# Cross attention on one core: output rows in other tiles, batch 0's sums in another order, and Wv loaded by halves of its columns

## The chip, the cores and the metric

The kernel runs on one core of a Trainium2 chip. The metric is the device time of one execution in microseconds (us). "Before" is the median of three runs, 992.72 us (991.76 to 993.55).

A core has five engines with queues of their own, each working in its queue's order: TensorE (PE in the profile; its weight loads are PEld), VectorE (DVE), ScalarE (ACT), GpSimd (POOL) and SyncE (SP), which here only issues DMAs. ACT and POOL issue some DMAs too. TensorE writes its results into PSUM banks, from which VectorE or ScalarE must copy them before the bank is used again.

## What is computed

There are 16 batches of 100 query rows of 640 columns (x) and 722 context rows of 384 columns. The last 4 context rows are the "ca" tokens; the other 718 are "enc". There are 8 heads of 80 columns. Cut to what matters:

```python
query = hidden_states @ Wq                  # 100 x 640
keyt, valt = enc @ Wk, enc @ Wv             # 718 x 640
hs = _mha(query, keyt, valt)
ca_q1 = jnp.einsum('btc,th->bch', ca, Wq_ca)[:, indices, :]
ca_hs1 = _mha(ca_q1, residual, residual)    # 100 queries on the batch's own x
ca_q2 = ca_hs1 @ Wq
ca_hs2 = _mha(ca_q2, ca @ Wk_ca, ca @ Wv_ca)
out = (hs + ca_hs2) @ Wout + b_out + residual
```

## The kernel before

Everything is float32. A loop of 16 steps handles one batch each, as a pipeline: in step b the scores, softmax and weighted values of batch b are computed, the keys of batch b + 1 are prepared, and the output rows that batch b - 1 has completed are projected with Wout. From the loop on, the order on TensorE, VectorE and GpSimd is the order in which the lines stand in the program; ACT's instructions are placed by the tile framework, with some tied behind a named instruction (`tc.issue_after`).

**Start.** Before the loop SP loads enc of batch 0, the small weights, Wq transposed, x, Wk transposed (into `kT`, L210) and Wq (into `wq_in`, L215), in that order. ACT issues Wv's four DMAs (L195): the first 128 rows in two halves of 320 columns, the other two blocks of 128 rows whole.[...] TensorE first computes the values of batch 0 (`first_values`, L277), then a fold of Wq with the token keys (L841, L864), transposes Wk (L886) and computes batch 0's keys (`first_keys`, L446). VectorE rearranges Wq into `wq_sb` (L897 to L904), and copies half of the transposed Wk into `wk_sb` (L889).

**Values and keys by blocks.** From batch 1 on a value or key product is made by the class `Blocks` with eleven block products instead of twelve, on sums and differences of the operands. It has two halves: `first_half` issues four products into four PSUM banks; the first bank is copied by ACT (L317), the others are added to that copy by VectorE (L319, L321, L323). `second_half` adds seven products into the same banks, with one ACT copy (L333) and three VectorE sums (L335, L337, L339). Key blocks `ka` and `kb` write `kT`; `last_keys` (L446) makes the fifth chunk, in two banks that `ka` has used.

**Scores and softmax.** `scores` (L505) makes the scores of 718 keys x 800 columns (8 heads x 100 queries) in three groups of PSUM banks; ACT copies them into `st` (L515). The greatest score of a column over all keys is found by VectorE (`larger`, then class `Maximum`): a transpose (L548), three reductions (L550, L553, L560), a spreading copy (L571 on ACT in two pieces, or L576 on VectorE) and a transpose back (L579). `subtract` (L976) takes it off the three pieces of `st`; `exponential` (L986) follows on ACT. The same class serves the first attention of the tokens (`softmax1`, on `e1`, with L663 and the exponential L667).

**Weighted values and the end of a step.** For each half g of the heads TensorE multiplies `st` with the values (L1117), 48 products into one bank `a_ps`, in two column tiles (64 and 36 queries). VectorE divides by the sums (L1125, L1127), which frees the bank, and adds the tokens' part `hs2` (L1133). `hs2` is made by GpSimd in `values2` (L736, L743), which is made to wait for the last subtraction of the step. Batch 1's second group of scores reuses the two `a_ps` banks of batch 0.

**Batch 0's step** (L996 to L1049) has an order of its own, because no batch stands before it: `Maximum` up to its third stage, `ka.first_half`, the rest of `Maximum`, the first subtraction, `kb.first_half`, two more subtractions, the second halves, `last_keys`, `values2`, and then the whole of `second.softmax1` and its exponential, all ahead of the division of batch 0's own result.

**Output rows.** `OC` (L32) cuts the 1600 output rows into tiles: eleven of 128 rows, one of 92 (rows 1408 to 1499) and one of 100 (the last batch). A tile is projected in the step after the one that completes it. `Last.transpose` transposes a batch's 100 rows (L780) and ACT copies them into the tile's `hsT` (L789); two `hsT` buffers exist. `Last.load` loads x's rows into `xn` and GpSimd adds the bias (L771). `Last.project` (L804) has ten products of 320 columns for a tile, VectorE adds `xn` (L816) and SP stores (L822; for the last tile each half by itself, L820). Step 15 projects two tiles of batch 14; after it the last batch's tile is projected with five chunks of 128 columns, of which the first two are transposed before the last head's products (L1114).

Of the kernel before, what the change touches and what calls it, by code (L numbers as in the profile page):

```python
# [8 lines left out]
F32 = mybir.dt.float32  # L9
AF = mybir.ActivationFunctionType  # L10
ALU = mybir.AluOpType
# [3 lines left out]
B, S, H = 16, 100, 640  # L15
# [3 lines left out]
P = 128  # L19
HC = H // P  # L20
CC = CAD // P
# [7 lines left out]
ROWS = NH * S  # L29
NB = ROWS // 32  # L30

OC = [(r, min(P, (B - 1) * S - r)) for r in range(0, (B - 1) * S, P)] + [((B - 1) * S, S)]  # L32
HT = NH * T

QC = [(0, 64), (64, S)]
# [10 lines left out]
for h in range(NH):  # L46
    lo = h * D
    while lo < (h + 1) * D:
        c = lo // P
        hi = min((h + 1) * D, (c + 1) * P)  # L50
        PIECES.append((h, c, lo - h * D, lo - c * P, hi - lo))
        lo = hi
# [39 lines left out]
def kernel(  # L92
# [18 lines left out]
    nc = tc.nc  # L111
# [4 lines left out]
    main = ctx.enter_context(tc.tile_pool(name="main", bufs=1))  # L116
# [7 lines left out]
    def psum4(name, n=4):  # L124
        return [
            ps4.tile([P, 512], F32, tag="ps4", name=f"{name}_{j}") for j in range(n)
        ]
# [15 lines left out]
        return main.tile([P, H], F32, tag="hs", name=name)  # L143

    def hsT_tile(name):
        return main.tile([P, HC, P], F32, tag="hsT", name=name, bufs=2)

    def xn_tile(name):
        return main.tile([P, H], F32, tag="xn", name=name, bufs=3)
# [41 lines left out]
    enc = enc_tile("enc_0")  # L191
    for c in range(CC):
        in_order(nc.sync.dma_start(out=enc[0][:, c, :P], in_=enct[0][:, c, :P]))
        for cols in [slice(0, H // 2), slice(H // 2, H)] if c == 0 else [slice(0, H)]:
            nc.scalar.dma_start(  # L195
                out=wv_sb[:, c, cols], in_=wv[c * P : (c + 1) * P, cols]
            )
# [553 lines left out]
    hsTs = {}  # L751

    class Last:
# [7 lines left out]
        def load(self):  # L761

            self.xn = {}
            for r, (lo, n) in enumerate(OC):
                if not self.b * S < lo + n <= (self.b + 1) * S:
                    continue
                xn = self.xn[r] = xn_tile(f"xn_{r}")
                nc.sync.dma_start(
                    out=xn[:n], in_=x.rearrange("b s n -> (b s) n")[lo : lo + n]
                )  # L770
                nc.gpsimd.tensor_tensor(xn[:n], xn[:n], bias[:n], ALU.add)  # L771

        def transpose(self, chunks=[(0, HC)]):
            b, hs = self.b, self.hs
# [19 lines left out]
        def project(self, chunks=range(HC)):  # L794
            for r, xn in self.xn.items():
                lo, n = OC[r]
                if chunks[0] == 0:
                    if self.split:
                        self.o_ps = [psum1(f"o_ps_{r}_{k}") for k in range(2)]
                    else:  # L800
                        self.o_ps = psum4(f"o_ps_{r}", 2)
                o_ps = self.o_ps
                for c, k in [(c, k) for k in range(2) for c in chunks]:
                    nc.tensor.matmul(  # L804
                        o_ps[k][:n, : H // 2],
                        hsTs[r][:, c, :n],
                        wout_sb[:, c, k * (H // 2) : (k + 1) * (H // 2)],
                        start=(c == 0),
                        stop=(c == HC - 1),
                    )  # L810
                if chunks[-1] < HC - 1:
                    continue
                o_v = out.rearrange("b s n -> (b s) n")[lo : lo + n]
                for k in range(2):
                    cols = slice(k * (H // 2), (k + 1) * (H // 2))
                    nc.vector.tensor_tensor(  # L816
                        xn[:n, cols], o_ps[k][:n, : H // 2], xn[:n, cols], ALU.add
                    )
                    if self.split:
                        nc.sync.dma_start(out=o_v[:, cols], in_=xn[:n, cols])  # L820
                if not self.split:
                    nc.sync.dma_start(out=o_v, in_=xn[:n])  # L822

    act, dve = nc.scalar.copy, nc.vector.tensor_copy

# [125 lines left out]
    for b in range(B):  # L951
# [32 lines left out]
        def exponential(i, behind):  # L984
            with tc.issue_after(behind.ins):
                return nc.scalar.activation(st[i], st[i], AF.Exp, scale=SCALE)  # L986
# [36 lines left out]
        if b == 0:  # L1023
            now.scores2()
            now.softmax3()
            for i, halves in ((3, (0, 1)), (5, (0,)), (5, (1,))):
                first_values(i, e_in, (act, act), halves)
            second.scores1()
            weight_sums([wv2[:, j] for j in range(3)], wv_raw, [3])
            second_next, enc_next = loads()  # L1030
            ka, kb = (key_blocks(b + 1, i, enc) for i in range(2))
            top = Maximum(most, f"{b}", lambda: copied)
            top.go(3)
            ka.first_half(psum4(f"room1_{b}"))
            top.go()
            subtract(0)
            exponential(0, top.spreading)
            kb.first_half()
            subtract(1)
            exponential(1, kb.copies[0])  # L1040
            less = subtract(2)
            ka.second_half()
            exponential(2, ka.copies[1])
            kb.second_half()
            final = last_keys(b + 1, enc)
            now.values2(less)
            second.load()
            second.softmax1()
            second.exponentials1(final[-1])  # L1049
        else:  # L1050
            last.transpose()
            va, vb, vc = (values(b, i, e_in) for i in range(NP))
            top = Maximum(most, f"{b}", lambda: va.copies[1])
            if b + 1 < B:
                second.scores1(seen)
                last.load()
                ka, kb = (key_blocks(b + 1, i, enc) for i in range(2))
            else:
                last.load()
                mine.load()  # L1060
            va.first_half()
            top.go(2)
            vb.first_half(psum4(f"room_{b}"))
            top.go(1)
            va.second_half()
            now.scores2()
            vb.second_half(lambda: top.spreading, top.go)
            subtract(0)
            vc.first_half()
            exponential(0, vc.copies[0])  # L1070
            now.softmax3()
            if b == B - 1:
                now.values2()
            subtract(1)
            if b + 1 < B:
                ka.first_half(psum4(f"room1_{b}"))
                less = subtract(2)
                vc.second_half()
                second_next, enc_next = loads()
                exponential(1, vc.copies[1])  # L1080
                ka.second_half()
                exponential(2, ka.copies[1])
                now.values2(less)
                second.load()
                last.project()
                kb.first_half()
                second.softmax1(3)
                final = last_keys(b + 1, enc)
                kb.second_half()
                second.softmax1()  # L1090
                second.exponentials1(kb.copies[1])
            else:
                exponential(1, vc.copies[0])
                subtract(2)
                last.project()
                vc.second_half()
                exponential(2, vc.copies[1])
# [10 lines left out]
        for g in range(2):  # L1108
            a_ps = psum1(f"a_ps_{b}_{g}")
            a_v = a_ps[:S, : 4 * (D + 1)].rearrange("p (h e) -> p h e", e=D + 1)  # L1110
            for h in range(4 * g, 4 * g + 4):
                if b == B - 1 and h == NH - 1:

                    mine.transpose([(0, 2)])  # L1114
                for i in range(len(KC)):
                    for lo, hi in QC:
                        nc.tensor.matmul(  # L1117
                            a_v[lo:hi, h % 4],
                            st[i // 2][:, i % 2, h * S + lo : h * S + hi],
                            block(i, h // 4)[:, h % 4],  # L1120
                            start=(i == 0),
                            stop=(i == len(KC) - 1),
                        )
            rs = small.tile([S, 4], F32, tag="rs", name=f"rs_{b}_{g}")
            nc.vector.reciprocal(rs.unsqueeze(2), a_v[:, :, D : D + 1])  # L1125
            cols = slice(4 * g * D, 4 * (g + 1) * D)
            nc.vector.tensor_tensor(  # L1127
                hs[:S, cols].rearrange("p (h d) -> p h d", h=4),
                a_v[:, :, :D],
                rs.unsqueeze(2).to_broadcast([S, 4, D]),  # L1130
                ALU.mult,
            )
            added = nc.vector.tensor_tensor(  # L1133
                hs[:S, cols], hs[:S, cols], hs2[:, cols], ALU.add
            )
        last = mine

    last.project(range(2))
    last.transpose([(2, HC)])
    last.project(range(2, HC))  # L1140


# [48 lines left out]
```

## Time and profile before

| what | us |
|---|---|
| median of three runs | 992.72 |
| the profiled execution | 992.88 |
| its span | 991.2 |
| VectorE busy, TensorE granted clock over the span | 666.9, 1.00 |
| start of batch 0's weighted values (a_ps) and of batch 1's scores | 97.38, 104.27 |
| weighted values of batch 15: start | 973.56 |
| end of the last TensorE instruction | 987.48 |

Times in the profile are counted from the span's start. A line of the timeline gives start, duration, engine, line of the program, operation, output and inputs, sizes and count; in brackets stands how long the engine was idle before it and what released it. A float32 product appears as two matmul records and two weight loads. The chain of waits is followed back from the last instruction: at each step to what released it. A list of waits gives the waiting instruction, what it waited for, the total, the number of times and the longest.

### The profile page before, as it was taken

Reading aid. Unit: us, or ns where it says so; the run is one execution under the profiler, and the core shown is the slowest. Engines: PE = TensorE matmul, PEld = TensorE weight load, DVE = VectorE, ACT = ScalarE, POOL = GpSimd, SP = SyncE. Lnnn points to the kernel's source line nnn. Section 1 sums busy time; section 2 is a strip of 40 time slices with the busy share of each in tenths; the row PEclk is TensorE's granted clock in tenths of the full one; section 3 lists DMA queues with packets and bytes.
Section 4 is the critical chain, followed back from the end, with each engine's and each line's share of the span. In section 5 each row is a group of like instructions: output and inputs, shape, how many; then the busy total and the mean of one; then the engine's idle time right before and its main releaser. Section 6 shows DMA issues by size and latency. Waiting matters only on the chain.

```text
span 991.2 us, 25050 instructions
## 1 busy us (share of the span) xinstructions
PE 980.1 (99%) x10945; PEld 747.5 (75%) x10945; DVE 666.9 (67%) x1229; ACT 312.9 (32%) x599; POOL 489.4 (49%) x439
## 2 busy tenths in 40 slices
PE   8999999999999999999999999999999999999998
PEld 6785869677696777868678686886869778696775
DVE  1358893967739587576946768468683876739782
ACT  1243342414334143333313233132332424324241
POOL 4467762565606546272653717446471564704513
PEclk9999999999999999999999999999999999999999
DMA  8651111120302202011120211102021030200101
GB/s 270 205 155 58 44 51 44 40 101 9 112 3 73 70 8 87 24 65 58 52 68 24 80 42 52 68 23 84 12 77 43 8 110 2 84 29 1 44 2 34
DMA packets 18015, 59.93 MB, mean 60 GB/s; under 512 B 2126, under 2 KB 8278, under 8 KB 14386
## 3 DMA queue, kind: packets, MB, share of 16 engines
q1 hardware_dynamic: 14658, 40.46, 12.6%
q0 software_dynamic: 2512, 16.72, 5.4%
q8 instruction: 86, 1.41, 0.6%
q10 hardware_dynamic: 736, 1.15, 0.4%
q14 instruction: 23, 0.19, 0.1%
HBM read 54.07 MB, written 4.26 MB: 59 GB/s over the span
## 4 chain that ended last, share of the span: by engine, by line
PE 93%; DMA 2%; SPq 1%; DVE 1%; POOL 1%; issue 1%; ACT 0%; ACTq 0%; DVEq 0%; POOLq 0%
PE room L302 19%; PE v_ps L302 18%; PE s_ps L505 12%; PE a_ps L1117 10%; PE k_ps L302 10%; PE o_ps L804 7%; PE kT_ps L446 7%; PE q_ps L420 7%; PE y_ps L611 2%; SPq L210 1%; DMA wq<-in_wq 1%; PE z_ps L674 1%; PE hst_ps L780 1%; PE v_ps L277 1%; DMA wv_sb<-in_wv 1%
## 5 line engine op out<-in xcount | busy, mean ns | idle before, releaser
L646 POOL TENSOR_TENSOR e<-ca,g 100x800 f32<-100x800 f32 x64 | 97.8, 1538 | 317.1 <-PE v_ps L302 299.3
L736 POOL TENSOR_TENSOR hs<-vb,p 100x640 f32<-100x640 f32 x64 | 83.8, 1320 | 132.9 <-DVE st L976 100.9
L302 PE MATMUL v_ps<-wv_sb,enc 128*128 128x320 f32 (+1 forms) x480 | 149.1, 433 | 0.0
L515 ACT COPY st<-s_ps 128x400 f32<-128x400 f32 (+1 forms) x192 | 80.5, 505 | 120.8 <-PE s_ps L505 120.8
L302 PEld LDWEIGHTS v_ps<-wv_sb,enc 128*128 128x128 f32 (+1 forms) x480 | 84.9, 179 | 41.1
L1117 PEld LDWEIGHTS a_ps<-v,st 128*64 128x64 f32 (+3 forms) x3072 | 109.0, 125 | 7.1 <-issue 6.5
L1117 PE MATMUL a_ps<-v,st 128*64 128x81 f32 (+3 forms) x3072 | 112.0, 233 | 0.7 <-issue 0.7
L986 ACT ACTIVATE st<-st 128x1600 f32<-128x1600 f32 (+1 forms) x48 | 73.8, 1538 | 103.2 <-DVE st L976 103.2
L976 DVE TENSOR_TENSOR st<-st,over 128x1600 f32<-128x1600 f32 (+1 forms) x48 | 105.3, 2197 | 0.0
L505 PE MATMUL s_ps<-qp,kT 32*128 32x100 f32 (+1 forms) x3072 | 98.5, 263 | 1.7 <-DVE hs L1127 1.1
L505 PEld LDWEIGHTS s_ps<-qp,kT 32*128 32x128 f32 (+1 forms) x3072 | 95.4, 179 | 3.7 <-issue 2.3
L653 POOL TENSOR_TENSOR e<-e,e 100x800 f32<-100x800 f32 x48 | 90.3, 1881 | 3.8
L302 PE MATMUL k_ps<-enc,wk_sb 128*128 128x359 f32 x240 | 82.6, 465 | 1.3 <-ACT v L284 1.0
L302 PE MATMUL room<-enc,wk_sb 128*128 128x359 f32 x240 | 82.2, 464 | 0.0
L991 DVE TENSOR_TENSOR most<-most,st 128x800 f32<-128x800 f32 (+1 forms) x64 | 64.4, 1007 | 25.6 <-ACT st L515 24.5
L743 POOL TENSOR_TENSOR hs<-hs,hs 100x640 f32<-100x640 f32 x48 | 73.9, 1540 | 3.8
L302 PE MATMUL room<-wv_sb,enc 128*128 128x320 f32 x240 | 74.4, 432 | 0.0
L804 PE MATMUL o_ps<-wout_sb,hsT 128*128 128x320 f32 (+2 forms) x260 | 72.2, 433 | 0.5 <-ACT hsT L789 0.5
L420 PEld LDWEIGHTS q_ps<-xT,wq_sb 128*128 128x128 f32 x400 | 67.9, 190 | 2.1 <-issue 0.5
L420 PE MATMUL q_ps<-xT,wq_sb 128*128 128x200 f32 x400 | 69.1, 333 | 0.0
L446 PE MATMUL kT_ps<-enc,wk_sb 128*128 128x359 f32 x210 | 68.8, 465 | 0.1
L1125 DVE RECIPROCAL rs<-a_ps 100x4 f32<-100x4 f32 x32 | 5.8, 181 | 92.1 <-PE a_ps L1117 91.9
(134 smaller groups left out, 1537.0 us busy)
## 6 DMA issues: line engine op xcount, KB each, us to landing
enc<-in_enct SPq DMA_DIRECT2D x15, 1077.0 KB
vb<-va_d POOLq DMA_DIRECT2D x16, 1000.0 KB, 6.7
xT<-in_xt SPq DMA_DIRECT2D x8, 500.0 KB
xn<-in_x SPq DMA_DIRECT2D x11, 320.0 KB
out<-xn SPq DMA_DIRECT2D x11, 320.0 KB
ca<-in_cas SPq DMA_DIRECT2D x16, 156.2 KB
wout_sb<-in_wqt SPq DMA_DIRECT2D x1, 1600.0 KB
wq<-in_wq SPq DMA_DIRECT2D x5, 320.0 KB
```

The source lines that it names most:

```text
L302: nc.tensor.matmul(bank[: left.shape[1], : right.shape[1]], left, right, start=(first and i == 0), stop=(last and i == len(products) - 1), ...
L420: nc.tensor.matmul(q_ps[:, : 2 * S].rearrange("p (j s) -> p j s", j=2), wq_sb[:, c, n * P : (n + 1) * P], xT[:, :, c, :], start=(c == 0), ...
L446: nc.tensor.matmul(k_ps[:, :KH], w, a, start=(c == 0), stop=(c == CC - 1))
L505: nc.tensor.matmul(s_ps[r][:n, 256 * a + lo : 256 * a + hi], kT[rows, c, k : k + n], rhs, start=(a == 0 and c == 0), stop=(c == HC - 1), s ...
L515: copied = nc.scalar.copy(st[:, :, 2 * r * S : 2 * (r + 1) * S], s_ps[r][:n].rearrange("p (a q) -> p a q", a=2)[:, :, : 2 * S],)
L646: first = nc.gpsimd.tensor_tensor(to, self.ca[:, t, :].unsqueeze(1).to_broadcast([S, NH, S]), g[:, :, t].unsqueeze(2).to_broadcast([S, NH, ...
L653: nc.gpsimd.tensor_tensor(e, e, to, ALU.add)
L736: first = nc.gpsimd.tensor_tensor(to, vb[:S, t, :].rearrange("p (h d) -> p h d", h=NH), p2[:, :, t].unsqueeze(2).to_broadcast([S, NH, D]), ...
L743: nc.gpsimd.tensor_tensor(sums, sums, to, ALU.add)
L804: nc.tensor.matmul(o_ps[k][:n, : H // 2], hsTs[r][:, c, :n], wout_sb[:, c, k * (H // 2) : (k + 1) * (H // 2)], start=(c == 0), stop=(c == ...
L976: less = nc.vector.tensor_tensor(st[i], st[i], top.over[:n].unsqueeze(1).to_broadcast([n, 2, ROWS]), ALU.subtract,)
L1117: nc.tensor.matmul(a_v[lo:hi, h % 4], st[i // 2][:, i % 2, h * S + lo : h * S + hi], block(i, h // 4)[:, h % 4], start=(i == 0), stop=(i = ...
```

## The change

Four things are changed.

1. *Output tiles.* `OC` becomes eleven tiles of 128 rows, one of 64 (rows 1408 to 1471) and one of 128 (rows 1472 to 1599, of which 28 are batch 14's). The tile of 64 is projected in a new function, `project_few`: each chunk's product of 640 columns is made as two of 320, in two column tiles of 64, alternating, into the lower and upper half of one bank; `xn` holds the two halves of its columns in the same way. `hsT` gets a third buffer.
2. *The end.* The last tile is projected with one chunk, not two, before the remaining transposes, and the second chunk follows them.
3. *Batch 0.* `kb.first_half` moves ahead of the rest of `Maximum`, whose spreading copies on ACT are tied behind `kb`'s first copy; the exponentials are tied behind the spreading copy; `softmax1` for batch 1 is cut in two, the second part behind the first half of batch 0's division; `hs2` is added once, for all columns, behind both divisions.
4. *Wv.* It is loaded in six DMAs, three of the first 320 columns and then three of the others. In the built program TensorE's first six products then go by halves too: three of the first half, three of the second.

```diff
-OC = [(r, min(P, (B - 1) * S - r)) for r in range(0, (B - 1) * S, P)] + [((B - 1) * S, S)]
+
+OC = [(r, P) for r in range(0, B * S - P - 64, P)] + [(B * S - P - 64, 64), (B * S - P, P)]
...
-        return main.tile([P, HC, P], F32, tag="hsT", name=name, bufs=2)
+        return main.tile([P, HC, P], F32, tag="hsT", name=name, bufs=3)
...
     for c in range(CC):
         in_order(nc.sync.dma_start(out=enc[0][:, c, :P], in_=enct[0][:, c, :P]))
-        for cols in [slice(0, H // 2), slice(H // 2, H)] if c == 0 else [slice(0, H)]:
+    for cols in slice(0, H // 2), slice(H // 2, H):
+        for c in range(CC):
             nc.scalar.dma_start(
                 out=wv_sb[:, c, cols], in_=wv[c * P : (c + 1) * P, cols]
             )
...
-                nc.sync.dma_start(
-                    out=xn[:n], in_=x.rearrange("b s n -> (b s) n")[lo : lo + n]
-                )
-                nc.gpsimd.tensor_tensor(xn[:n], xn[:n], bias[:n], ALU.add)
+                rows = x.rearrange("b s n -> (b s) n")[lo : lo + n]
+                for at, cols in self.parts(n):
+                    to = xn[at : at + n, : cols.stop - cols.start]
+                    nc.sync.dma_start(out=to, in_=rows[:, cols])
+                    nc.gpsimd.tensor_tensor(to, to, bias[at : at + n, cols], ALU.add)
+
+        def parts(self, n):
+
+            if n > 64:
+                return [(0, slice(0, H))]
+            return [(64 * k, slice(k * (H // 2), (k + 1) * (H // 2))) for k in range(2)]
...
+                if n <= 64:
+                    self.project_few(r, xn)
+                    continue
...
+        def project_few(self, r, xn):
+            lo, n = OC[r]
+            (o_ps,) = psum4(f"o_ps_{r}", 1)
+            for c in range(HC):
+                for at, cols in self.parts(n):
+                    nc.tensor.matmul(
+                        o_ps[at : at + n, : H // 2],
+                        hsTs[r][:, c, :n],
+                        wout_sb[:, c, cols],
+                        start=(c == 0),
+                        stop=(c == HC - 1),
+                    )
+            nc.vector.tensor_tensor(
+                xn[:, : H // 2], o_ps[:, : H // 2], xn[:, : H // 2], ALU.add
+            )
+            o_v = out.rearrange("b s n -> (b s) n")[lo : lo + n]
+            for at, cols in self.parts(n):
+                nc.sync.dma_start(out=o_v[:, cols], in_=xn[at : at + n, : H // 2])
...
-            top = Maximum(most, f"{b}", lambda: copied)
+            top = Maximum(most, f"{b}", lambda: kb.copies[0])
             top.go(3)
             ka.first_half(psum4(f"room1_{b}"))
+            kb.first_half()
             top.go()
             subtract(0)
             exponential(0, top.spreading)
-            kb.first_half()
             subtract(1)
-            exponential(1, kb.copies[0])
+            exponential(1, top.spreading)
             less = subtract(2)
...
-            second.softmax1()
-            second.exponentials1(final[-1])
+            second.softmax1(4)
...
+            if b == 0 and g == 1:
+                second.softmax1()
+                second.exponentials1(final[-1])
...
-            added = nc.vector.tensor_tensor(
-                hs[:S, cols], hs[:S, cols], hs2[:, cols], ALU.add
-            )
+            if b:
+                nc.vector.tensor_tensor(hs[:S, cols], hs[:S, cols], hs2[:, cols], ALU.add)
+        if b == 0:
+            nc.vector.tensor_tensor(hs[:S], hs[:S], hs2, ALU.add)
...
-    last.project(range(2))
+    last.project(range(1))
     last.transpose([(2, HC)])
+    last.project(range(1, 2))
     last.project(range(2, HC))
```

## The prediction

> **What bounds the kernel now.** I read the page first: engine shares, then the chain that ended last.
>
> ```profile
> PE 980.1 (99%) x10945; PEld 747.5 (75%) x10945; DVE 666.9 (67%) x1229; ACT 312.9 (32%) x599; POOL 489.4 (49%) x439
> PE 93%; DMA 2%; SPq 1%; DVE 1%; POOL 1%; issue 1%; ACT 0%; ACTq 0%; DVEq 0%; POOLq 0%
> ```
>
> TensorE (PE) carries 93% of the chain. So time comes only from TensorE work taken away or from one of its few waits. Next I asked for TensorE's waits over the whole span. Of the eight in the list, these four touch what the change edits (columns: total us, times, longest):
>
> ```profile
> PE s_ps L505 <- DVE hs L1127: 1.1, 1, 1.1
> PE k_ps L302 <- ACT v L284: 1.0, 1, 1.0
> PE v_ps L277 <- DMA wv_sb<-in_wv: 0.9, 1, 0.9
> PE o_ps L804 <- ACT hsT L789: 0.5, 1, 0.5
> ```
>
> Two lie in batch 0, one at the start, one at the very end. The chain in order of time says whether they matter at the start and the end:
>
> ```profile
> 21.00 11.66 DMA wq<-in_wq
> 32.68 0.50 DVE wq_sb L897 x2
> 33.70 18.38 PE kT_ps L446 x60
> ...
> 980.92 2.33 PE o_ps L804 x8
> 983.55 0.42 ACT hsT L789
> 984.01 3.49 PE o_ps L804 x12
> ```
>
> TensorE's start at 33.70 hangs on the first Wq piece, landed at 32.66, not on Wv. At the end the ACT copy of the transposed rows sits bare between two groups of matmuls. Last, the timelines of batch 0 by engine:
>
> ```profile
> 82.36 0.86 ACT L571 COPY spread<-mx 64x800 f32<-64x800 f32 x1 [3.99 <-DVE mx L560]
> 83.13 0.41 ACT L284 COPY v<-v_ps 103x320 f32<-103x320 f32 x1
> 86.13 1.88 POOL L653 TENSOR_TENSOR e<-e,e 100x800 f32<-100x800 f32 x1
> 86.69 3.00 DVE L976 TENSOR_TENSOR st<-st,over 128x1600 f32<-128x1600 f32 x1
> 91.32 3.55 DVE L976 TENSOR_TENSOR st<-st,over 128x1600 f32<-128x1600 f32 x2
> 94.79 0.53 DVE L335 TENSOR_TENSOR kT<-room,kT 128x359 f32<-128x359 f32 x1
> 94.95 2.50 POOL L736 TENSOR_TENSOR hs<-vb,p 100x640 f32<-100x640 f32 x2 [4.54 <-DVE st L976]
> 97.38 6.97 PE L1117 MATMUL a_ps<-v,st 128*64 128x81 f32 x192
> 104.05 1.85 DVE L663 TENSOR_TENSOR e<-e,over 100x800 f32<-100x800 f32 x1
> 108.28 0.99 PE L505 MATMUL s_ps<-qp,kT 32*128 32x100 f32 x25 [1.07 <-DVE hs L1127]
> ```
>
> A value copy (L284) stands behind the first spread copy in ACT's queue; the three score subtractions (L976) are interrupted by the second key block's sums (L319 to L323, 89.62 to 91.40); GpSimd's hs2 (L736 on) starts when the last subtraction ends and runs to 105.05; the DVE add that needs it (L1133) stands ahead of the evacuation (L1127) that batch 1's scores wait for.
>
> [...]the L976 at 86.69 took 3.00 us, against 1.81 for one at 958.73 with GpSimd idle; 88.01 (end of L653) + 1.8 = 89.8.[...] 192 records of a_ps in 6.90 us are 36 ns each, where 320 columns take 269 ns in o_ps (5.38 us for 20 records), so 81 columns alone would take 68.[...]
>
> **The change, part by part.** The sum is made against the profiled execution: 992.88 us, a span of 991.2 and 1.7 around it. Outside the start, batch 0, batch 15 and the end, the instruction order of every engine is the same in both programs.
>
> *Wv by halves.* TensorE now does c = 0, 1, 2 of the first half, then of the second. Before, it stood 0.87 us (to 7.05) for the whole of c = 1, when 640 KB of Wv had landed. After, the third piece is 480 KB deep; between 3.64 (first piece) and 6.92 (640 KB) that reads as about 5.7, when TensorE, at 1.07 us a matmul there, wants it (5.8); the fourth comes at about 6.9, as it is wanted. So it gains about 0.9 us at 11 us. But then VectorE reaches L897 at 31.5 and not 32.36, and waits for the Wq piece either way; wk_sb (L889) and kT_ps follow. Bytes ahead of Wq are the same; 288 packets more[...] are 18 per engine. ACT's queue has two DMAs more at about 0.45 us, ahead of nothing until 10.63. SP's queue: in the changed program xT waits for the fourth Wv piece, at the same depth as the piece it waited for (6.92). Bound from both sides: −0.3 (Wq a little earlier) to +0.5 (18 packets[...]). I take 0.
>
> *Batch 0.* VectorE: mx is done at 82.34 as before; ACT has by then done the value copy and both c22 copies (k_ps's is ready at 81.0), so TensorE's wait at 83.6 goes. Six kT sums at 0.62 follow to 86.1, the transpose L579 to 87.1; L976 waits for GpSimd until 88.0 (as it did) and ends at 89.75. GpSimd's waiting L363 (0.7) goes next, by the alternation seen at 962 to 967, then L976 twice at 1.8: 90.45 to 94.05, against 94.87 before. So only 0.8 comes of three sums moved[...]. The first L335 ends at 94.6 against 95.32; kT_ps's second half waits for that bank; a_ps starts at 96.6, a gain of 0.77. exp(2) ends near 95.85, and a_ps first reads it at 96.9. TensorE itself would be ready a microsecond sooner; that wait stays.
>
> After that, a_ps ends at 103.5. VectorE: six L335 to 97.1, softmax steps to 102.2 (5.1, as before), rs and L1127 of the first half to 102.9, L579 to 103.95, L663 held by GpSimd's last hs2 sum to 104.2, done 105.2, second rs and L1127 to 105.9. Batch 1's scores want that bank at 103.5 + 2.4 + 0.3 = 106.2: no wait, where 1.07 to 1.28 stood. The whole-row add L1169 costs 1.0, after it, in front of L1010, which waits for ACT until 108 anyhow; cover 1 us. ACT's e1 exponential comes at 105.3, ahead of 105.99. Sum: 0.77 + 1.1 = **1.9**; bounds 1.0 (L335 as late as before[...]) and 3.3 (both waits ahead of a_ps gone too). Batch 1 shows no TensorE wait from 116.17 to 173, so it passes on.
>
> *Output tiles.* In batch 15 the 92-row tile (10 matmuls, 20 records at 269 ns, 5.38 us) becomes 64 rows in two column tiles, 10 pairs of records at about 270 ns: 2.7. Gain **2.7**, bounds 0 (no overlap) and 2.7. What is late next? vc's second half starts at 967.1; its L333 copy frees ACT at 968.7; exp(2), whose subtraction ended 967.24, runs to 970.25; a_ps starts at 970.9 (before 973.56). Cover: 0.6. GpSimd's hs2 still ends at 975.92, so the first L1133 is done at 976.5; the transposes want it at 970.9 + 6.04 = 976.95. Cover 0.4; without it that much is lost. A third hsT copy on ACT at 945.7 (0.3) has VectorE behind it busy until 947.65. The third hsT buffer only removes a reuse wait. GpSimd's bias adds are 4 for 3, same columns.
>
> *The end.* From a_ps's end T: before, four matmuls (2.15), transposes to T + 2.55, copy to T + 3.0, twelve records to T + 6.55. After: two matmuls to T + 1.0, transposes when L1133 is done (T + 1.28, as measured) to T + 1.8, two matmuls over the copy to T + 2.85, twelve records to T + 6.25: 0.3. The last stores have 128 rows for 100[...]: −0.1 to +0.3, taken as 0. **0.3**.
>
> **Sum**: 1.9 + 2.7 + 0.3 = 4.9; 992.88 − 4.9 = 988.0 for an execution like the profiled one, which is 0.16 above the median of the runs: 987.8.
>
> **Rivals.**
> - *Batch 0 gives little*: the kT sums ahead of the spreading transpose[...] eat what the order gains, and batch 1's scores wait again behind L663. For it: all of this hangs on margins of 0.3 us. Against: the add and its GpSimd wait are gone from ahead of L1127. About 0 to 0.5 in place of 1.9: 989.4 to 989.9; at the worst 990.2.
> - *Column tiles don't overlap*: 320 columns are longer than any seen in pairs. 2.7 lost: 990.5. Against: 36 ns per a_ps record.
> - *More*: all waits before a_ps go (3.3) and the start moves a little (0.3): 986.1.
> - *Slower: the second half of Wv comes late.* Its last two pieces wait, in ACT's queue, for the semaphores of the first enc piece and the first Wv piece. If they land x after TensorE wants them (8 to 9 us), x less the 0.9 gained and the 0.3 slack at 32.4 goes on the path. From x = 6.1 it eats all; at 10 it is 8.8 late: 987.8 + 8.8 = 996.6. Against: those semaphores are there by about 3.7, and DMA moved 0.65 MB between 6 and 8 us.
>
> **How the numbers follow.** Forecast 0.67, little from batch 0 0.13, no overlap 0.05, more 0.11, slower 0.04. The range 986.2 to 990.3 takes in the forecast's bounds, the first rival and most of the third. What can be told from no change is 0.2%, 2 us (990.7 and 994.7): faster 0.87 (the forecast, the first and third whole, part of the second), same 0.09, slower 0.04.
>
> **What would show it.** After: a first o_ps group of 20 records and then a 64-row group in about 2.7 us; a_ps of batch 0 about 0.8 us earlier; no wait of s_ps for L1127; kT_ps still starting near 33.7, after Wq; no bare ACT copy in the chain's end. Wrong: kT_ps over a microsecond off, a new TensorE wait ahead of batch 15's a_ps or of its transposes, or 64-row records at 269 ns each.

## The result, and the profile after

| | median of the runs | range |
|---|---|---|
| before | 992.93 us (9 runs) | 991.76 to 993.94 |
| after | 990.05 us (9 runs) | 988.77 to 991.36 |

The ratio is 0.9969, with a 95% interval of 0.9958 to 0.9979: 2.9 us faster, where 4.9 to 5.1 were forecast. The profiled execution of after took 991.36 us (span 989.6), the longest of the nine, so 1.3 us of its time over their median are its own. None of the nine reached the forecast's 987.8.

From the page after, the engine shares and the chain that ended last:

```profile
PE 978.3 (99%) x10945; PEld 746.6 (75%) x10945; DVE 666.2 (67%) x1227; ACT 313.5 (32%) x600; POOL 487.0 (49%) x440
PE 95%; DMA 2%; SPq 1%; DVE 1%; issue 1%; ACT 0%; ACTq 0%; DVEq 0%
```

The chain has gone from 93% to 95% TensorE, and "issue" is still there. TensorE's waits after, whole span (columns: total us, times, longest):

```profile
PE s_ps L507 <- issue: 2.8, 2, 1.5
PE a_ps L1147 <- issue: 1.2, 1, 1.2
PE kT_ps L448 <- DVE wk_sb L920: 0.8, 1, 0.8
PE y_ps L613 <- ACT st L517: 0.7, 1, 0.7
PE v_ps L304 <- DVE v L321: 0.6, 1, 0.6
```

All four waits that the prediction showed of before are gone. In their place stand three of "issue", in which TensorE waited for nothing that the profile shows. The list of before had two such rows already (`s_ps` 0.7, `a_ps` 0.7) among its ten, not eight, rows, and the prediction passed them over. The last three rows are new waits too, of 0.6 to 0.8 us: at the start, in batch 8 (533.60) and in batch 4. The chain after, from batch 0's scores to batch 1's (start us, us, what):

```profile
61.30 5.13 PE s_ps L507 x154
66.44 1.52 issue
67.95 4.35 PE s_ps L507 x69
72.30 0.68 PE z_ps L676 x56
...
97.51 6.90 PE a_ps L1147 x191
104.41 6.37 PE s_ps L507 x206
110.79 1.25 issue
112.03 1.22 PE s_ps L507 x31
```

Before, the scores of batch 0 had no break:

```profile
62.49 7.28 PE s_ps L505 x240
```

Here they took 11.0 us. Only 1.52 of the 3.7 more is the gap: behind it 69 records take 4.35 us (the same 69 take 2.74 in a kernel below, all but Wv). The table by stretches says why (us, TensorE busy, PEclk, DMA share, GB/s):

```profile
62.00:66.00 4.00, 4.00 (x137) 1.00 0.67 224
66.00:68.00 2.00, 0.48 (x10) 1.00 0.00 0
68.00:70.00 2.00, 2.00 (x51) 0.71 0.07 16
70.00:72.00 2.00, 2.00 (x42) 0.50 0.00 0
```

The granted clock falls to half behind the gap. Also to be seen: a DMA share of 0.67 just ahead of the gap and none in it.

At the start and at the end:

```profile
19.46 12.01 DMA wq<-in_wq
31.49 0.50 DVE wq_sb L928 x2
31.99 0.48 DVE wk_sb L920
32.51 7.51 PE kT_ps L448 x24
```

`kT_ps` starts 1.19 us earlier, because Wq was issued at 19.46 and not at 21.00. Whether Wv's order did that is a question for the experiments.

```profile
960.70 5.38 PE o_ps L816 x20
966.09 2.84 PE o_ps L841 x20
```

and before

```profile
959.03 10.77 PE o_ps L804 x40
```

The 64-row tile is 20 records in 2.84 us, 142 ns each, where one of the 40 records before took 269 ns: the column tiles overlap. The bare ACT copy of the end is gone.

So the tiles, the end and batch 0's order did in place what they were to do, and most of what is missing lies in gaps that no wait explains. The rest is about these.

### The profile page after: what moved, and what is told of

Its sections match the earlier page's. It is cut to its first block, busy times and chain, and to the rows that moved or that the text cites. A ratio compares the mean times of both kernels' runs of the same rounds, so it can differ in the third digit from the quotient of the medians.

```text
span 989.6 us, 25057 instructions
## 1 busy us (share of the span) xinstructions
PE 978.3 (99%) x10945; PEld 746.6 (75%) x10945; DVE 666.2 (67%) x1227; ACT 313.5 (32%) x600; POOL 487.0 (49%) x440
## 3 DMA queue, kind: packets, MB, share of 16 engines
q8 instruction: 86, 1.41, 0.6%
## 4 chain that ended last, share of the span: by engine, by line
PE 95%; DMA 2%; SPq 1%; DVE 1%; issue 1%; ACT 0%; ACTq 0%; DVEq 0%
PE room L304 19%; PE v_ps L304 18%; PE s_ps L507 12%; PE a_ps L1147 11%; PE k_ps L304 10%; PE kT_ps L448 7%; PE q_ps L422 7%; PE o_ps L816 6%; PE y_ps L613 2%; DMA wq<-in_wq 1%; SPq L212 1%; PE z_ps L676 1%; PE hst_ps L789 1%; PE v_ps L279 1%; DMA wv_sb<-in_wv 0%
## 5 line engine op out<-in xcount | busy, mean ns | idle before, releaser
L648 POOL TENSOR_TENSOR e<-ca,g 100x800 f32<-100x800 f32 x64 | 99.2, 1561 | 320.3 <-PE v_ps L304 248.6
L816 PE MATMUL o_ps<-wout_sb,hsT 128*128 128x320 f32 x240 | 66.8, 433 | 0.0
```

Source lines behind the costliest of these rows:

```text
L648: first = nc.gpsimd.tensor_tensor(to, self.ca[:, t, :].unsqueeze(1).to_broadcast([S, NH, S]), g[:, :, t].unsqueeze(2).to_broadcast([S, NH, ...
L816: nc.tensor.matmul(o_ps[k][:n, : H // 2], hsTs[r][:, c, :n], wout_sb[:, c, k * (H // 2) : (k + 1) * (H // 2)], start=(c == 0), stop=(c == ...
```

## First experiments: the parts alone

**Tiles and end alone** (`OC`, `parts`, `project_few`, the third hsT buffer and the last three calls of after, put into before).

```diff
-OC = [(r, min(P, (B - 1) * S - r)) for r in range(0, (B - 1) * S, P)] + [((B - 1) * S, S)]
+OC = [(r, P) for r in range(0, B * S - P - 64, P)] + [(B * S - P - 64, 64), (B * S - P, P)]
...
-    last.project(range(2))
+    last.project(range(1))
     last.transpose([(2, HC)])
+    last.project(range(1, 2))
```

> The kernel before with the output tiles and the end of the change alone (64 rows in two column tiles, the third hsT buffer, the order of the last matmuls). Recorded prediction: 2.7 + 0.3 = 3.0 us faster, kT_ps still at 33.7. Rival 1 (the tiles overlap only partly, or give back in batch 15): 1.5 to 2 us faster. Rival 2 (the tiles give 3.0 and the missing two microseconds of the whole change are lost at the start or in batch 0): 3.0, as recorded, and then the other parts together give nothing.

Measured: 989.47 us beside 993.30 of before; ratio 0.9967 (0.9955 to 0.9978), 3.3 us faster by the ratio. That is as much as the whole change gains. And `kT_ps` started at 32.62, with Wv loaded as before.

**Batch 0 alone.**

```diff
-            top = Maximum(most, f"{b}", lambda: copied)
+            top = Maximum(most, f"{b}", lambda: kb.copies[0])
...
+            kb.first_half()
             top.go()
...
-            second.softmax1()
-            second.exponentials1(final[-1])
+            second.softmax1(4)
...
+            if b == 0 and g == 1:
+                second.softmax1()
+                second.exponentials1(final[-1])
```

and the one add for all columns behind both divisions.

> The kernel before with the new order of batch 0 alone. Recorded prediction: 1.9 us faster (0.8 ahead of a_ps, 1.1 for the wait of batch 1's scores). Rival 1 (what the order gains is given back in later batches[...]): 0 to 1 us faster, with a_ps of batch 0 0.8 or more earlier but z_ps of batch 8 no more than 1 earlier. Rival 2: the part is worth its 1.9 and the loss belongs to the earlier start: then 1.9 here, and the change without Wv is faster than the whole change.

Measured: 993.12 us; ratio 0.9996 (0.9988 to 1.0005). No gain to be told from nothing, and the upper end of it is 1.2 us. Its chain in batch 1's scores:

```profile
102.11 6.37 PE s_ps L505 x206
108.49 2.29 issue
110.78 1.75 PE s_ps L505 x31
```

The wait for L1127 is gone, as it was to be, and a gap of 2.29 us stands at the same place as after's: behind 206 records, 31 before the end. Its clock by stretches:

```profile
108.00:110.00 2.00, 0.49 (x14) 1.00 0.03 8
110.00:112.00 2.00, 1.22 (x34) 0.83 0.00 0
112.00:114.00 2.00, 2.00 (x75) 0.50 0.03 8
```

Its 14 executions fall into two groups by their mean granted clock: seven at 1.0 have a median of 992.21 us, six at 0.998 one of 994.21. Of 31 executions of before in the same series, three are at 0.998, and the 19 at 1.0 have a median of 993.07: among executions at the full clock the reorder is worth 0.9 us, and the slow clock takes it back in six of the fourteen.

**Wv alone.**

```diff
-        for cols in [slice(0, H // 2), slice(H // 2, H)] if c == 0 else [slice(0, H)]:
+    for cols in slice(0, H // 2), slice(H // 2, H):
+        for c in range(CC):
```

> The kernel before with Wv by halves of its columns alone. Recorded prediction: 0, kT_ps at 33.7. Rival 1 (the start moves and passes on): kT_ps near 32.5 and 1.2 us faster. Rival 2 (the start moves, and a gap of some 1.5 us in batch 0's scores with the slow clock behind it takes it back): kT_ps near 32.5, z_ps of batch 0 no earlier than 62.5 + 7.3, and a time from the same to 2 us slower.

Measured: 992.44 us; ratio 0.9995 (0.9986 to 1.0004). `kT_ps` at 32.83.

**All but Wv** (the same edit taken back in after).

> The changed kernel with Wv loaded as before; all else of the change stays. Recorded prediction: 4.9 us faster than before, so about 988, and about 2 us faster than the whole change. Rival 1 (Wv's part is worth its 1.2 us at the start): 1.2 us slower than the whole change, about 991.2. Rival 2 (Wv's part costs through the gap in batch 0's scores): no gap over a microsecond in s_ps at 67 to 70, and 1 to 2.5 us faster than the whole change.

Measured: 989.91 us; ratio 0.9967 (0.9956 to 0.9979), the same as the whole change; `kT_ps` at 32.85. Two gaps together of 0.76 in batch 0 (66.52 and 70.13) and one of 1.25 in batch 1 (108.73). None of the three expected times came: the gap in batch 0's scores is small, as the second rival had it, but the kernel is no faster.

What follows: Wv does not cause the gaps, and no effect of it on the start is shown: over all profiles here `kT_ps` starts anywhere from 32.11 to 33.74 with the old order of Wv, and from 32.20 to 33.74 with the new. The 33.70 of before's profile was one draw from that. The tiles have their gain. The question is batch 0: its two waits are gone and the time isn't.

## What TensorE waits for: the instruction queue

The page's list of DMA queues has two of kind "instruction", before and after: q8, with 86 packets and 1.41 MB (16 KB each), and q14, with 23 packets and 0.19 MB. I take q8 for the queue of TensorE's instructions. That is an estimate from the page: TensorE's 10945 matmul records and as many weight loads are 21890 of the 25057 instructions of after, and 255 for each of the 86 packets. At two instructions for a matmul with its weight load, and with 240 records of `s_ps` without a gap in 7.27 us, 30 ns each, a packet of 255 would last 3.9 us there; the packets of q8 do start 3.9 us apart in dense scores (103.10 and 106.95 in an experiment below). In after the DMA view of 108 to 112 us (slices of 0.1 us):

```profile
DMA  5950598039900000600000000000000000000000
GB/s 205 1024 205 0 205 819 307 0 102 410 307 0 0 0 0 0 164 0 0 0 0 0 0 0 0 0 0 0 0 0 0 0 0 0 0 0 0 0 0 0
q0 software_dynamic: 49, 0.36, 25.7%
q8 instruction: 1, 0.02, 1.6%
```

q0 is GpSimd's queue: the rest of batch 1's 1 MB load of `vb`, issued at 104.23, whose last packets start at 109.2 and end at 109.67 (the view counts a packet where it starts). The one instruction packet starts at 109.66, right behind them (16 KB in a slice of 0.1 us are the 164 GB/s). TensorE ran dry at 110.79 and went on at 112.03, 2.4 us after the packet's start. So I put these side by side, for batch 1's scores (us; the packet is the first of q8 over 1 us after the scores' start):

| kernel | s_ps starts | packet after it | gap | packet to end of gap |
|---|---|---|---|---|
| after | 104.41 | 5.2 | 1.25 | 2.4 |
| all but Wv | 102.36 | 5.1 | 1.25 | 2.5 |
| batch 0 alone | 102.11 | 6.1 | 2.29 | 2.5 |
| before | 104.27 | 6.0 | 0.66, behind the wait of 1.07 | 2.4 |

And in batch 0's scores of after: packet at 65.64, gap until 67.95, 2.3 us. All thirteen profiles of this document together have 27 gaps of over 0.2 us, from 34 us on, that TensorE's waits put down to issue; every one ends 2.3 to 2.8 us after the start of a packet of q8.

The theory: while a `vb` load is under way (DMA share 0.67 from 62 to 66 us in after, 0.55 from 108 to 110), the next packet of q8 starts late, and the later it starts, the longer the gap. In before, the lines of batch 1's scores behind the wait for L1127 are

```profile
108.28 3.76 PE s_ps L505 x106
112.04 0.66 issue
```

The packet was as late there as in batch 0 alone (6.0 and 6.1 us from the scores' start), but TensorE, held up by the wait, came to the place of the gap, 31 records before the end, 7.8 us after the scores' start and not 6.4, and the gap was 0.66 and not 2.29. But a load under way is not enough: in batch 0 of before, where `vb` was issued at 62.20 and not 59.78, packets started at 64.06 and 67.48, within the load (63.5 to 69.3), and there was no gap. Why a load should delay one packet until its end and not another, no run shows.

## Experiments on the loads

**Both loads moved.** Nothing but two DMA issues changes place in GpSimd's queue; all other engines have the same order.

```diff
         if b == 0:
-            now.load()
...
             weight_sums([wv2[:, j] for j in range(3)], wv_raw, range(3))
+            now.load()
...
             second.copy()
+        if b == 1:
+            now.load()
...
             now.values2(less)
-            second.load()
             second.softmax1(4)
```

> The changed kernel with two 1 MB loads of vb moved in GpSimd's queue: batch 0's from ahead of the scores to behind the weight sums (about 71 us instead of 59.8), batch 1's from ahead of batch 1's scores to behind the encoder sums (about 111 us instead of 104.2). Nothing else moves. Theory (while a vb load fills the DMA engines, TensorE's next 16 KB of instructions come late; it stands until 2.5 us after that packet starts): no gap in s_ps or z_ps over 0.2 us up to 118 us, no instruction packet at the end of the load, 1.25 us from batch 1's scores and 0.7 or more from batch 0's, so about 988 and no run with a mean clock under 0.999. Rival 1 (the fetch is late whatever else the DMA engines do): gaps at the same two places, 990. Rival 2 (the loads only move the gaps to where they now lie): gaps in v_ps or room, 989.5 to 990.5.

Measured: 985.09 us (984.54 to 985.70) beside 992.68 of before; ratio 0.9923 (0.991 to 0.9937). All five executions have a granted clock of 1.0. The loads were then issued at 68.49 and 107.92. The chain and the DMA view from 100 to 108 us (slices of 0.2 us):

```profile
100.70 7.27 PE s_ps L507 x240
107.97 0.68 PE z_ps L676 x56
```

```profile
DMA  0000000000000003000000000000000000300000
q8 instruction: 2, 0.03, 1.9%
```

The scores run through, with packets 2.4 and 6.2 us after their start, where after's first came at 5.2. One gap of 0.10 us is left in batch 0 (68.79). The gain was expected at 2 us and is 5.0 by the medians, or 4.6 by the ratios of the two series: the expectation counted gaps alone, not the slow clock behind them nor a later loss, for which see the section on batch 4. Between the two profiled executions (989.6 and 983.0 us) the difference can be placed: 4.0 us up to batch 0's `z_ps` (0.3 of it at the start, the rest gap and slow clock), 1.25 from there to batch 1's, 0.98 in batch 4 and 0.7 in batch 8; the other batches give back 0.3.

**Batch 1's load alone moved.**

> The changed kernel with batch 1's vb load alone moved behind the encoder sums. Theory: the gap of 1.25 us in batch 1's scores goes, the one in batch 0's scores stays with its slow clock in some executions: 1.2 us faster than the changed kernel, about 988.8. Rival 1: the gap stays, 990.

Measured: 987.56 us; ratio 0.9948 (0.9936 to 0.9961). The gap in batch 1 is gone, one of 0.82 at 66.50 in batch 0 stays. That is 2.5 us by the medians where 1.2 was expected, and all five executions are at a clock of 1.0, where some slow ones were expected; why the gain was twice the expected one is not shown. By the medians each load is worth about half.

**The kernel before with both loads moved, and the same with batch 0's new order.** These two price the reorder with the loads out of the way.

> The kernel before with both vb loads moved in the same way. Theory: it has a gap of 0.66 us in batch 1's scores (after the wait of 1.07 for VectorE[...]) and in some executions one of 0.4 to 0.8 in batch 0's: 0.7 to 1.3 us faster than before, about 992. The wait of s_ps for L1127 stays (1.1). Rival 1: 993, gaps where they were.

> The kernel before with both vb loads moved and the new order of batch 0 alone. Theory (the reorder is worth its 1.9 us once the fetch no longer takes back the 1.1 that the wait for L1127 gave): 1.9 us faster than the kernel before with the loads moved, about 990, and no gap at batch 1's scores, where the reorder alone showed 2.29 us and a slow clock. Rival (the reorder is worth little in itself): within 0.7 us of the kernel before with the loads moved.

Measured: 990.48 us, ratio 0.9977 (0.9967 to 0.9986), and 988.39 us, ratio 0.9958 (0.9946 to 0.9971). The reorder is worth 2.1 us here; alone in before it was worth 0.2 (993.30 to 993.12). The first gained more than the 0.7 to 1.3 expected; its wait of `s_ps` for the evacuation (L1127 before, L1128 there) shrank to 0.6 as well, probably because GpSimd no longer spends 0.6 us on issuing the load just ahead of that add. It keeps a wait of 0.2 on issue in `z_ps` with no `vb` load near, and three of its nine executions have a clock of 0.997 to 0.999. And after's wait of 0.66 in `y_ps` of batch 8, put down to ACT, also ends 2.4 us after a packet, with no other DMA between 526 and 536 us. Not every such wait is explained.

**Wv as before, with the loads moved.**

> The changed kernel with both vb loads moved (985.1 us) and Wv loaded as before. Recorded prediction (Wv by halves is worth 0, kT_ps waits for Wq either way): 985.1. Rival (the old order of Wv lets TensorE's own chain of v_ps end later than Wq, as four of six profiles with the old order have it; kT_ps began at 32.62 to 33.74 there against 32.20 to 32.83 with the new): kT_ps 0.3 to 1 later and 985.5 to 986.1. With the reorder of batch 0 and the loads moved at 988.4, the output tiles and the end are then worth 988.4 less this time: 3.0 by the recorded prediction.

Measured: 985.47 us (984.65 to 985.79); ratio 0.9912 (0.9897 to 0.9928). By the medians that is 0.4 over the kernel with the new order, by the ratios 1.1 under it (0.9912 and 0.9923); the ranges and the intervals overlap, and the two come from different series, with before at 993.50 in this one and 992.68 in the other. `kT_ps` began at 32.11, not later than with the new order, against the rival. No worth of Wv's order is shown. For the tiles and the end the same two readings are 2.9 and 4.6 us; within the one series, 988.39 to 985.09, they and Wv together are worth 3.3.

**A third load moved.** Batch 11's load is issued at 690.88 in after, ahead of batch 10's `a_ps`.

```diff
-        if b == 1:
+        if b in (1, 11):
             now.load()
...
                 now.values2(less)
-                second.load()
+                if b != 10:
+                    second.load()
```

> The changed kernel with both vb loads moved (985.1 us) and, the same way, the load of batch 11, which lies ahead of batch 10's a_ps (issued at 690.9 in the changed kernel, TensorE stands 1.17 to 1.25 us at 697.8). Theory: the gap in a_ps goes, 1.2 us faster, about 983.9. Rival (that gap belongs to the position in the instruction stream, not to the load): it stays, 985.1.

Measured: 984.25 us (983.75 to 984.45); ratio 0.9900 (0.9882 to 0.9917). With two loads moved, the chain at batch 10's `a_ps` reads

```profile
685.28 5.77 PE a_ps L1148 x157
691.05 1.25 issue
692.30 1.46 PE a_ps L1148 x34
```

and with three

```profile
686.54 6.90 PE a_ps L1149 x191
693.43 6.63 PE s_ps L507 x217
```

The gap goes, and the interval from batch 10 to 11 falls by 1.6 us (table below). The two times come from different series: the gain is 0.8 us by the medians and 2.3 by the ratios, with 1.2 expected. The list of TensorE's waits then holds no row of "issue". The moved load now runs under batch 11's scores (data from 692.4 to 697.2 us) and makes no gap there: again a load under way is not enough. This version is faster than both kernels: by 0.8 to 1.2% than before, and its median is 5.8 us under after's.

**The two loads issued by SP in place of GpSimd**, at the same places.

```diff
-            nc.gpsimd.dma_start(
+            (nc.sync if b < 2 else nc.gpsimd).dma_start(
                 out=vb[:S],
```

> The changed kernel with the same two vb loads at the same places, but from SP's queue in place of GpSimd's; bytes and time are alike. Theory (it is the transfer that the instruction packet queues behind, whoever issued it): the gaps in s_ps stay, about 990. Rival (it is GpSimd's queue that goes ahead of the instructions): the gaps go, about 985.5 to 986.5.

Measured: 988.86 us; ratio 0.9955 (0.9939 to 0.9972): neither number. Its chain:

```profile
62.09 5.13 PE s_ps L507 x154
67.22 2.37 issue
69.59 4.38 PE s_ps L507 x69
...
106.08 7.27 PE s_ps L507 x240
```

Batch 0's gap is there, with half the clock behind it (0.54 from 70 to 72), so the gap doesn't hang on GpSimd's queue alone. Batch 1's is gone: there the packet came 3.0 us after the scores' start, in the middle of the load. The two loads are not alike in time, as the expectation had it: SP's moved its 100 packets of 10 KB in 5.8 us (105.9 to 111.7), GpSimd's the same packets in 4.1 (105.5 to 109.7 in after), and SP's began 0.2 us ahead of the scores, GpSimd's 1.1 behind their start. So the run changes the rate and the place of the load with its queue. Which of them decides, it doesn't say.

## A later loss: VectorE beside GpSimd in batch 4

The starts of `z_ps` in TensorE's timeline give the length of each batch. Four intervals of them (us, one execution each):

| kernel | 0 to 1 | 1 to 2 | 4 to 5 | 10 to 11 |
|---|---|---|---|---|
| before | 44.15 | 59.56 | 56.49 | 52.08 |
| batch 0 alone | 43.51 | 60.51 | 57.46 | 52.61 |
| after | 40.96 | 59.56 | 57.47 | 52.60 |
| before, both loads moved | 42.46 | 59.56 | 56.48 | 52.47 |
| batch 0 alone, both loads moved | 39.37 | 59.57 | 56.48 | 52.20 |
| after, both loads moved | 39.69 | 59.59 | 56.49 | 52.67 |
| after, three loads moved | 39.37 | 59.94 | 56.49 | 51.10 |

The column 4 to 5 has two values, 0.98 apart (to 0.03). The higher one appears in all five kernels that have batch 0's reorder and batch 0's load at its old place (beside the two in the table: all but Wv, 57.45; batch 1's load alone moved, 57.48; SP's loads, 57.49), in none of the other eight, and none of the edits touches batch 4. The timelines of that place, first after, then after with both loads moved, 5.2 us earlier:

```profile
307.68 1.54 POOL L648 TENSOR_TENSOR e<-ca,g 100x800 f32<-100x800 f32 x1
307.84 1.42 DVE L712 TENSOR_TENSOR e<-s,mx 100x32 f32<-100x32 f32 x1
309.18 1.00 DVE L581 STREAM_TRANSPOSE over<-spread 128x800 f32<-128x800 f32 x1
```

```profile
302.64 0.19 DVE L712 TENSOR_TENSOR e<-s,mx 100x32 f32<-100x32 f32 x1
302.75 1.00 DVE L581 STREAM_TRANSPOSE over<-spread 128x800 f32<-128x800 f32 x1
302.79 1.54 POOL L648 TENSOR_TENSOR e<-ca,g 100x800 f32<-100x800 f32 x1
```

A subtraction of 32 columns (L712) takes 0.19 us if it comes 0.15 ahead of GpSimd's product (L648), and 1.42 if it comes 0.16 behind it, when it ends at 309.26, just after the product (309.22). Here a sixth of a microsecond decided it. The transpose behind it is late, and TensorE's wait of 0.6 for `v` (L321) follows. What moves GpSimd by 0.3 us four batches on, I haven't followed; that the loss comes and goes with these edits is seen in one profile of each kernel, its route isn't shown.

## Why the prediction was right, and where not

- *Bound and direction*: right. TensorE carries the chain, and only its waits and its work count.
- *Output tiles and end*, 2.7 + 0.3: right. 2.5 (two groups of 5.38 us became one of 5.38 and one of 2.84) and 0.4 (from the end of `a_ps` to TensorE's end, 6.14 us for 6.57) in the trace; 3.3 (2.2 to 4.5) as a part alone, and 3.3 together with Wv once the gaps are gone.
- *Wv*, 0: right for the time. The reason was right in part: Wq sets the start in after (0.8 us of waiting for L920 behind it). But the start "near 33.7" took one execution's number for the kernel's: unchanged loads gave 32.1 to 33.7.
- *Batch 0 ahead of a_ps*, 0.77: too small. From `v_ps` (L277) to `a_ps` before took 25.55 us (71.83 to 97.38), after 23.39 (74.12 to 97.51): 2.2, nearly the upper bound (3.3 less 1.1). "That wait stays" was wrong; TensorE waits for nothing in this stretch after. What was mis-sized is VectorE's delay beside GpSimd: the prediction held the end of the first subtraction, behind GpSimd's product at 88.0, for fixed. In after GpSimd's last product (L365) ended at 88.89, just as VectorE's three subtractions began (88.82), and they ran through in 5.30 us, where they took 3.00 and 3.55 before.
- *Batch 1's scores*, 1.1: this is the step that failed: "no wait, where 1.07 to 1.28 stood". The wait went, but a second wait stood 4 us behind it, the gap that ended 2.4 us after a late packet of q8. From `a_ps` to batch 1's `v_ps` the trace gives 18.79 and 17.99: 0.8 with all, and 0.6 more of it was lost to the gap (0.66 to 1.25). In batch 0 alone the gap was 2.29, and the slow clock came behind it. The prediction had put the "issue" rows of its own list at nothing.
- *"It passes on"*: not wholly. Batch 4 gave 0.98 back behind VectorE's late subtraction (1.42 us for 0.19), and in the profiled execution batch 8 another 0.6 (57.19 from `z_ps` to `z_ps` for 56.57).
- *Sum*: with the loads out of the way the change is worth 5.4 us (990.48 to 985.09), of which 2.1 are batch 0 and 3.3 the rest, where 1.9 and 3.0 were forecast. The kernel as it stands gains 2.5 less. Its profile shows the gaps, the slow clock and batch 4 in that place; how much each takes in a usual execution is not measured. The forecast had no term for them. That the time fell into the range, 0.25 us from its end, is luck: the range was that wide for other reasons.
- *The rival "batch 0 gives little"* came nearest in time (989.4 to 990.2), though not for its reasons: not the sums, not L663. Its 989.4 to 989.9 count from 988.0, the other rivals from 987.8; from 987.8 they are 989.2 to 989.7. The others didn't occur.

## What to carry to other kernels

A wait of "issue" in a stretch of many small matmuls is worth a look at the DMA queue of kind "instruction": ask for its packets, and for the large transfer that ends just before them. A 1 MB load whose data is wanted much later can be issued elsewhere (batch 0's in after: issued at 59.78, first read at 94.20); here three such moves, on top of the change, were worth more than the change itself. A cost may show in the interval from batch 1 to 2, which is up to 0.4 us longer in some of these kernels. Which places are harmless must be tried: a load under way made a gap in some dense stretches and none in others. And before a removed wait is booked as a gain, ask what else is late behind it: here the gap was 0.66 us behind the wait of 1.07 in before, and 2.29 without it in batch 0 alone.

## What the runs showed of the hardware

- A gap of 1.5 to 2.4 us in TensorE's work was followed by a stretch at half clock (after at 70, batch 0 alone at 112, SP's loads at 70), 3.4 us of it in the first two. That is worked out from the table by stretches: mean clocks of 0.71, 0.50 and 0.93 in the 2 us from 68, 70 and 72 in after make 3.4 us at half, those of 0.83, 0.50 and 0.82 from 110, 112 and 114 in batch 0 alone the same. Gaps of 1.25 us were not followed by it: the clock was 1.00 in the 2 us from 112 in after (gap at 110.8) and from 110 in all but Wv (108.7), and 1.0 over the whole execution with both loads moved (691). What the half clock cost in after was as large as the gap: 69 records took 4.35 us for 2.74.
- In dense stages TensorE stood up to 2.37 us (batch 0's scores with SP's loads) in a wait of "issue", and in all 27 gaps the next matmul came between 2.3 and 2.8 us after the start of a packet of q8.
- The changed kernel with both loads moved spread over 1.2 us in five executions (984.54 to 985.70), all at a clock of 1.0; before with both loads moved spread over 2.7 in nine (989.84 to 992.58), the two longest at 0.997 and 0.998.
